# The zero fill of a table in DRAM: four transfers behind the constants, or one transfer ahead of everything

## The chip, the cores and the metric

The kernel runs on one core of one Trainium2 chip. The metric is the device time of one execution in microseconds (us), as the median of several runs. A kernel here is a program for five engines, each with its own queue of instructions in a fixed order: PE (matrix products), DVE and ACT (vector and scalar work), POOL (GpSimd), and SP, which only issues transfers. ACT and POOL issue transfers too. All transfers run on the core's 16 DMA engines, and the engines meet through semaphores.

## The reference, cut to what matters

The reference is two layers of a network on a graph: 1250 nodes with 512 channels, 40000 edges with 8 attributes each, one per head. The part that matters here is the attention of the first layer, whose scores between a source node s and a target node d get a bias from the edges between them:

```
table[s, d, 0:8] = sum over edges e = (s, d) of exp(edge_attr_8[e, :] - shift)
table[s, d, 8]   = number of edges (s, d)
```

Pairs without an edge must read as zero (the attention masks them). Ahead of the attention, and beside the building of this table, another branch of the layer is computed from x alone: normalization, K, V and Q products, linear attention, a small feed-forward part.

## The kernel before, in words

Nodes are padded to 1280, which gives ten tiles of 128. The table is `adj`, in DRAM, with one row of 9 floats for each of the 1280 x 1280 pairs (58.98 MB) and 896 spare rows for values that belong nowhere. It is used in three steps.

*Zero fill* (lines 221 to 228). POOL writes a row `zrow` of 128 x 1800 zeros. SP then issues four transfers, each of which writes that row 16 times for each of 128 partitions (14.4 thousand KB each), and a small one for the spare rows. In the program's text this stands behind the constants.

*Keys and weights* (lines 230 to 297). ACT loads `src`, `dst` and the edge attributes `wgt`. DVE makes a key `src * 1280 + dst` of each edge. PE turns the keys in three blocks, and ACT stores them in DRAM (`key_d`, line 269), from where they come back spread over all partitions (`kr`, line 311). ACT takes the exponential of `wgt` (line 283), and DVE splits the result into three bf16 parts `w` (line 290 and on).

*Scatter* (generator `scatter_edges`, lines 303 to 393). Groups of six columns of 128 edges are compared with each other by key (DVE, lines 325 and 335), PE sums the weights of equal keys (line 317), and POOL adds each column's sums to the table by an indirect DMA (line 351), 313 in all. The first group's keys come by ACT's queue, all later ones by SP's. The main program calls `pump(n)` to put n groups between its other work. A column's sums have 32 buffers, so that DVE and PE may run ahead of POOL.

The other branch (from line 481 on) begins with the loads of x in ten tiles, `xn` (line 487), the weights `L_mix_Wk` and `L_mix_Wv` and the bias rows, all issued by ACT. DVE normalizes the tiles, PE turns them (line 168) and makes the K and V products (line 179) and their product `kvps` (line 527). In PE's order the first group of the scatter stands ahead of most of these products, and the second group behind the last of them.

After the scatter the attention loads the table in slabs of 128 sources (`slab`, line 656), the first of which waits for the last two batches of scatters.

What sets the order around the zero fill: a scheduler places the instructions on each engine from the program's text, and the order within an engine is then fixed. Each transfer of SP or ACT is given one of eight completion semaphores (0 to 7), whichever engine issues it. A transfer that gets a semaphore that another transfer had before it waits, in its engine's queue, until that earlier one has landed, and what stands behind it in this queue waits with it. In the built program of this kernel the first zero transfer has semaphore 7, and the next transfer with this semaphore is ACT's third store to `key_d`; zero transfers 2 to 5 have semaphores 6, 1, 2 and 3, and the second follows ACT's first store to `xb_d` on semaphore 6.

Of the kernel before, what the change touches and what calls it, by code (L numbers as in the profile page):

```python
# [11 lines left out]
F32 = mybir.dt.float32  # L12
# [10 lines left out]
P = 128  # L23
N = 1250
NP = 1280
NT = NP // P
TAIL = N - (NT - 1) * P
C = 512
KC = C // P
# [4 lines left out]
EC = EF + 1  # L34
EREM = E - EF * P
B = 3
G = 2 * B
W3 = 3 * (H + 1)
CH = H + 1
NKEY = NP * NP  # L40
NROW = NKEY + (G + 1) * P
# [5 lines left out]
NEXP = 8  # L47
TOPK = 16
NKEYS = 256
# [17 lines left out]
def tile_gps_layers(ctx: ExitStack, tc: tile.TileContext, a, out):  # L67
    nc = tc.nc
# [4 lines left out]
    dram = ctx.enter_context(tc.tile_pool(name="dram", bufs=1, space=DRAM))  # L73
# [6 lines left out]

    def ps_tr(shape=(P, 512), name="tr"):
        return psum.tile(list(shape), F32, tag="tr", bufs=2, name=name)


    ident = const.tile([P, P], F32, name="ident")
# [61 lines left out]
    def norm_stats(pool, x_t, eps, name):  # L147

        st = pool.tile([P, 6], F32, tag="ln_st", name=name + "st")
        nc.vector.bn_stats(st, x_t)  # L150
        mv = pool.tile([P, 2], F32, tag="ln_mv", name=name + "mv")
        nc.vector.bn_aggr(mv, st)
        return mv[:, 0:1], rsqrt(pool, mv[:, 1:2], [P, 1], eps, name)
# [10 lines left out]
    def transposed(dst, tiles, t, gain=None, shift=None):  # L164

        ps = ps_tr((P, KC, P))
        for c in range(KC):
            nc.tensor.transpose(ps[:, c, :], tiles[:, c * P:(c + 1) * P], ident)
        to = dst[:, :, t * P:(t + 1) * P]
        if gain is None:  # L170
            nc.any.tensor_copy(to, ps)
        else:
            for c in range(KC):
                nc.vector.tensor_scalar(to[:, c, :], ps[:, c, :], col(gain, c), col(shift, c),
                                        op0=OP.mult, op1=OP.add)
# [9 lines left out]
    def nodes_of(t):  # L185
        return TAIL if t == NT - 1 else P
# [6 lines left out]
        mm(ps, [(w[:, c, m * P:(m + 1) * P], xT[:, c, c0:c0 + cn]) for c in range(xT.shape[1])])  # L193


    adj = dram.tile([NROW, CH], F32, name="adj")
    key_d = dram.tile([EC, P], F32, name="key_d")
    cnt_d = dram.tile([NP, NP], F32, name="cnt_d")
    q_d = dram.tile([P, KC, NP], F32, name="q_d")
    xm_d = dram.tile([NP, C], F32, name="xm_d")  # L200
    xb_d = dram.tile([NP, C], F32, name="xb_d")
    att_d = dram.tile([P, KC, NP], F32, name="att_d")
    deg_d = dram.tile([P, NP], F32, name="deg_d")
    w1f_d = dram.tile([NEXP, P, KC, 256], F32, name="w1f_d")
    wgd_d = dram.tile([P, KC, C], F32, name="wgd_d")
    wqd_d = dram.tile([P, KC, NKEYS], F32, name="wqd_d")
    bsum_d = dram.tile([P, C], F32, name="bsum_d")

    s_xn = ctx.enter_context(ExitStack())
    pxn = s_xn.enter_context(tc.tile_pool(name="xn", bufs=1, side="right"))
    xn = pxn.tile([P, NT, C], F32, tag="xn", name="xn")

    s_edge = ctx.enter_context(ExitStack())
    pe = s_edge.enter_context(tc.tile_pool(name="edge", bufs=1, side="right"))
    s_tmp = ctx.enter_context(ExitStack())
    ptmp = s_tmp.enter_context(tc.tile_pool(name="edgetmp", bufs=1, side="right"))

    zrow = pe.tile([P, 1800], F32, name="zrow")
    nc.gpsimd.memset(zrow, 0.0)
    adj_p = adj[0:NKEY, :].rearrange("(p r) c -> p (r c)", p=P)
    step = 16 * 1800
    for z0 in range(0, NKEY * CH // P, step):
        nc.sync.dma_start(adj_p[:, z0:z0 + step].rearrange("p (a f) -> p a f", f=1800),
                            zrow[:, None, :].to_broadcast([P, 16, 1800]))
    nc.sync.dma_start(adj[NKEY:NROW, :].rearrange("(p r) c -> p (r c)", p=P), zrow[:, :(G + 1) * CH])  # L228

    def edge_column(name, src, width, dt, fill):  # L230
        t = ptmp.tile([P, EC, width] if width > 1 else [P, EC], dt, name=name)
# [31 lines left out]
    for c0 in range(0, EC, P):  # L263
        cn = min(P, EC - c0)
        ps = ps_tr((P, P))
        nc.tensor.transpose(ps[:cn, :], key[:, c0:c0 + cn], ident)
        kt = ptmp.tile([P, P], F32, tag="kt", name="kt", bufs=2)
        nc.vector.tensor_copy(kt[:cn], ps[:cn, :])
        nc.scalar.dma_start(key_d[c0:c0 + cn, :], kt[:cn])


    mx = pe.tile([P, H], F32, name="mx")
    nc.vector.tensor_reduce(mx, wgt.rearrange("p j h -> p h j"), axis=AX.X, op=OP.max)
    ps = ps_tr((P, P))
    nc.tensor.transpose(ps[:H, :], mx, ident)
    mxt = pe.tile([H, 1], F32, name="mxt")
# [204 lines left out]
    with (tc.tile_pool(name="mix", bufs=1) as pm, tc.tile_pool(name="mixw", bufs=2) as pw,  # L481
# [99 lines left out]
        for t in range(NT):  # L581
            ps = ps_mm()
            node_mm(ps, hid, t, w2)
            f = pw.tile([P, C], F32, tag="f", name="f")
# [20 lines left out]
    with tc.tile_pool(name="gqkv", bufs=2) as pq:  # L605
# [5 lines left out]
        for t in range(NT):  # L611
            z = pq.tile([P, C], F32, tag="z", name="z")
            m, r = norm_stats(pq, xn[:, t, :], 1e-5, "lnz")
# [220 lines left out]
    def node_norm(pool, t, x_t, eps, name):  # L834

        st = pool.tile([P, 6], F32, tag="nn_st", name=name + "st")
        nc.vector.bn_stats(st, x_t)
        mv = pool.tile([P, 2], F32, tag="nn_mv", name=name + "mv")
        nc.vector.bn_aggr(mv, st)
        w = pool.tile([P, 1], F32, tag="nn_w", name=name + "w")  # L840
        nc.vector.tensor_scalar_add(w, mv[:, 1:2], eps)
        s = pool.tile([P, 1], F32, tag="nn_s", name=name + "s")
        nc.scalar.activation(s, w, AF.Sqrt)
        r = pool.tile([P, 2], F32, tag="nn_r", name=name + "r")
        nc.vector.reciprocal(r[:, 0:1], s)
        nc.vector.tensor_scalar(s, r[:, 0:1], r[:, 0:1], w, op0=OP.mult, op1=OP.mult)
        nc.vector.tensor_scalar(s, s, -0.5, 1.5, op0=OP.mult, op1=OP.add)
        nc.vector.tensor_scalar(r[:, 0:1], r[:, 0:1], s, None, op0=OP.mult)
        nc.vector.tensor_scalar(r[:, 1:2], mv[:, 0:1], r[:, 0:1], -1.0, op0=OP.mult, op1=OP.mult)
        return r  # L850

    with tc.tile_pool(name="gff", bufs=1) as pf, tc.tile_pool(name="gffw", bufs=2) as pw:
# [34 lines left out]
        with tc.manual_schedule(engines={nc.tensor.engine, nc.vector.engine, nc.scalar.engine}):  # L887
            for t in range(NT + 2):
                if t < NT:
# [7 lines left out]
                    r = node_norm(pw, t, X[:, t, :], 1e-5, "lnf")  # L897
# [24 lines left out]
            for c, (c0, cn) in enumerate(CHUNKS):  # L922
                n = cn // P
                for k, t in enumerate(range(c0 // P, c0 // P + n)):
# [4 lines left out]
                    r = nodes_of(t)  # L929
# [1068 lines left out]
```

## Time and profile before

| what | value |
|---|---|
| median of 3 runs | 2404.56 us (2402.94 to 2405.39) |
| the profiled execution, its own time | 2411.48 us |
| its span, first to last instruction | 2409.0 us |
| mean granted TensorE clock | 0.908 |
| PE busy | 1979.6 us (82%) |
| DVE busy | 1511.0 us (63%) |
| ACT busy | 808.2 us (34%) |
| POOL busy | 697.1 us (29%) |
| written to DRAM / read from it | 92.80 MB / 161.05 MB |

The span is that of one profiled execution; the median is of other runs, without the profiler. The profile shows the busy time of each engine, cut into 40 slices of the span, the costliest groups of instructions (line, engine, operation, output and inputs, how often; busy time and mean ns of one; idle time just ahead of them and what ended most of it), and a chain of waits, followed back from the last instruction to what released each step. Timelines list instructions in order of time: start, length, engine, line, operation, and in brackets the idle time ahead of it and what ended that. "SPq" and "ACTq" are the queues of these engines, in which transfers are issued[...].

### The profile page before, as it was taken

Reading aid. Unit: us, or ns where it says so; the run is one execution under the profiler, and the core shown is the slowest. Engines: PE = TensorE matmul, PEld = TensorE weight load, DVE = VectorE, ACT = ScalarE, POOL = GpSimd, SP = SyncE. Lnnn points to the kernel's source line nnn. Section 1 sums busy time; section 2 is a strip of 40 time slices with the busy share of each in tenths; the row PEclk is TensorE's granted clock in tenths of the full one; section 3 lists DMA queues with packets and bytes.
Section 4 is the critical chain, followed back from the end, with each engine's and each line's share of the span. In section 5 each row is a group of like instructions: output and inputs, shape, how many; then the busy total and the mean of one; then the engine's idle time right before and its main releaser. Section 6 shows DMA issues by size and latency. Waiting matters only on the chain.

```text
span 2409.0 us, 29786 instructions
## 1 busy us (share of the span) xinstructions
PE 1979.6 (82%) x10588; PEld 1180.5 (49%) x10588; DVE 1511.0 (63%) x4838; ACT 808.2 (34%) x1529; POOL 697.1 (29%) x448
## 2 busy tenths in 40 slices
PE   0767698885498499999789999999999999978943
PEld 0335475552244366666444546667445445555521
DVE  3717958879961399999561456656222242599998
ACT  0000011110230277677441156666111122244653
POOL 2006888888888100000000000000000000036665
PEclk9987798986599599999899999999999999989975
DMA  9898565444542665665250110000400101000000
GB/s 359 361 418 239 111 125 110 86 61 88 136 72 16 231 223 186 233 211 196 86 175 26 43 36 1 1 1 13 153 26 27 35 3 68 22 22 10 10 9 17
DMA packets 134385, 255.79 MB, mean 106 GB/s; under 512 B 51805, under 2 KB 90134, under 8 KB 132572
## 3 DMA queue, kind: packets, MB, share of 16 engines
q1 hardware_dynamic: 82368, 234.11, 26.3%
q0 software_dynamic: 46512, 8.02, 7.1%
q10 hardware_dynamic: 5356, 11.77, 1.3%
q8 instruction: 83, 1.36, 0.2%
q14 instruction: 66, 0.54, 0.1%
HBM read 161.05 MB, written 92.80 MB: 105 GB/s over the span
## 4 chain that ended last, share of the span: by engine, by line
PE 53%; DVE 23%; DMA 7%; ACT 6%; POOL 4%; issue 3%; SPq 3%; ACTq 0%; DVEq 0%; POOLq 0%
PE mm L179 26%; POOL adj L351 4%; PE sc L682 4%; PE one L731 4%; DVE eqx L335 4%; ACT wT L722 3%; DVE eq L325 3%; PE one L721 2%; DMA adj<-tot,idx 2%; PE ag L1382 2%; PE sc L1061 2%; PE av L1115 2%; PE one L1102 2%; SPq L228 2%; DMA adj<-zrow 2%
## 5 line engine op out<-in xcount | busy, mean ns | idle before, releaser
L351 POOL DMA_INDIRECT adj<-tot,idx x313 | 500.5, 1599 | 276.9 <-DMA kr<-key_d 180.1
L711 DVE SCALAR_TENSOR_TENSOR ex<-ex,slab 128x1280 f32<-128x1280 f32 x80 | 197.1, 2503 | 0.0
L325 DVE SCALAR_TENSOR_TENSOR eq<-kr,key,upto 128x128 bf16<-128x128 f32 (+2 forms) x313 | 145.3, 475 | 65.6 <-DMA kr<-key_d 40.0
L1313 DVE SCALAR_TENSOR_TENSOR X<-mm,gate,X 128x512 f32<-128x512 f32 x80 | 60.0, 750 | 196.9 <-PE mm L179 196.8
L335 DVE TENSOR_SCALAR_CACHE_REDUCE eqx<-kr,key 128x384 bf16<-128x384 f32 (+1 forms) x312 | 175.5, 599 | 0.8 <-PE even L317 0.8
L1251 POOL MEMSET padded<- 128x128 f32 x3 | 0.5, 204 | 543.0 <-DVE faT L1136 543.0
L722 ACT COPY wT<-one 128x512 f32<-128x512 f32 (+1 forms) x240 | 116.0, 516 | 96.8 <-PE one L721 92.5
L721 PE MATMUL one<-ident,ex 128*128 128x128 f32 x800 | 127.6, 289 | 23.5 <-ACT wT L722 19.7
L179 PE MATMUL mm<-w,hT 128*128 128x512 f32 (+1 forms) x320 | 144.3, 603 | 0.0
L179 PE MATMUL mm<-faT,w 128*128 128x512 f32 (+1 forms) x384 | 140.2, 518 | 0.7 <-ACT bs L1135 0.7
L682 PE MATMUL sc<-kT,q 64*128 64x512 f32 (+1 forms) x480 | 106.2, 566 | 40.9 <-DMA q<-q_d 38.6
L692 DVE CUSTOM_DVE_ANT_0 ex<-sc,none 128x1280 f32<-128x1280 f32 x80 | 115.7, 1485 | 17.4 <-PE sc L682 16.4
L721 PEld LDWEIGHTS one<-ident,ex 128*128 128x128 f32 x800 | 86.0, 143 | 66.8 <-ACT wT L722 48.2
L1075 DVE CUSTOM_DVE_ANT_0 ex<-sc,cmask 128x512 f32<-128x512 f32 (+3 forms) x144 | 72.9, 560 | 66.3 <-PE sc L1061 66.2
L704 ACT ACTIVATE ex<-ex,low 128x1280 f32<-128x1280 f32 x80 | 104.7, 1360 | 10.7 <-DVE low L697 10.7
L317 PEld LDWEIGHTS <-eq 128*128 128x128 bf16 x625 | 43.0, 103 | 132.3 <-DVE eq L325 96.0
L668 POOL DMA_DIRECT2D deg_d<-cnt x10 | 8.4, 844 | 340.2 <-ACT attT L738 319.6
L179 PEld LDWEIGHTS mm<-faT,w 128*128 128x128 f32 x384 | 73.3, 192 | 66.9 <-issue 65.9
L731 PE MATMUL one<-wT,gva 128*64 128x128 f32 x1600 | 103.0, 287 | 3.5 <-ACT wT L722 1.9
L1307 ACT ACTIVATE hT<-mm,cols 128x512 f32<-128x512 f32 (+1 forms) x48 | 29.0, 607 | 217.4 <-PE mm L179 217.4
L731 PEld LDWEIGHTS one<-wT,gva 128*64 128x64 f32 x1600 | 93.3, 145 | 13.5 <-ACT wT L722 13.5
L179 PEld LDWEIGHTS mm<-w,hT 128*128 128x128 f32 (+1 forms) x320 | 61.2, 192 | 75.6 <-issue 75.6
(493 smaller groups left out, 4090.7 us busy)
## 6 DMA issues: line engine op xcount, KB each, us to landing
adj<-zrow SPq DMA_DIRECT2D x4, 14400.0 KB
slab<-adj SPq DMA_DIRECT2D x10, 5760.0 KB, 17.3
kr<-key_d SPq DMA_DIRECT2D x50, 576.0 KB, 4.4
cnt_d<-cnt SPq DMA_DIRECT2D x10, 640.0 KB
deg_d<-cnt POOLq DMA_DIRECT2D x10, 640.0 KB, 7.0
adjT<-cnt_d SPq DMA_DIRECT2D x5, 1280.0 KB
adj<-tot,idx POOLq DMA_INDIRECT x313, 3.3
fw<-in_L_ffn_W SPq DMA_DIRECT2D x8, 512.0 KB, 3.9
```

The source lines that it names most:

```text
L179: nc.tensor.matmul(ps, lhsT=l, rhs=r, start=i == 0, stop=i == len(pairs) - 1)
L325: nc.vector.scalar_tensor_tensor(eq[:, :n], kr[:, k0 * P:k0 * P + n], key[:, c0 + c:c0 + c + 1], upto[:, B - 1 - c:, :].rearrange("p c x - ...
L335: nc.vector.tensor_scalar(eq[:, :n * P], kr[:, k0 * P:(k0 + n) * P], key[:, c0 + c:c0 + c + 1], None, op0=OP.is_equal, op1=OP.add, accum_o ...
L351: st = nc.gpsimd.indirect_dma_start(out=adj, out_offset=bass.IndirectOffsetOnAxis(ap=idx[:, c:c + 1], axis=0), in_=tot[:, c, :], in_offset ...
L682: nc.tensor.matmul(sc[e][:, d0:d0 + dn], lhsT=q[half(e), m, :], rhs=kT[half(e), m, d0:d0 + dn], start=True, stop=True)
L692: nc.vector.tensor_tensor_reduce(out=ex, in0=sc[e][:, :NP], in1=none, scale=-0.125, scalar=-LOWEST, op0=OP.add, op1=OP.min, accum_out=low[ ...
L704: nc.scalar.activation(exs[e], exs[e], AF.Exp, bias=low[:, e:e + 1], scale=-1.0)
L711: nc.vector.scalar_tensor_tensor(exs[e], exs[e], 1.0, sl[:, :, hd], op0=OP.mult, op1=OP.mult, accum_out=den[:, hd:hd + 1])
L721: nc.tensor.transpose(ps[:, k, :], weights[t, m][e][:, (d0 + k) * P:(d0 + k + 1) * P], ident)
L722: nc.scalar.copy(wT[:, d0:d0 + dn, :], ps[:, :dn])
L731: nc.tensor.matmul(av[half(e), 0, :], lhsT=va[:, d, hd * D:(hd + 1) * D], rhs=turned[e][:, d, :], start=d == 0, stop=d == NT - 1)
L1075: nc.vector.tensor_tensor_reduce(out=exs[e][:, d0:d0 + dn], in0=sc[k][e][:, :dn], in1=cmask[:, NP - n + d0:NP - n + d0 + dn], scale=-0.125 ...
```

## The change: what it does

The row `zrow` is written by DVE as its first instruction, the four transfers become one that SP issues, and the small one for the spare rows goes to ACT. All of this, with the DRAM tiles and the two pools that it needs, moves in the text ahead of the constants. The size of the table, the row and the number of bytes stay as they are.

```diff
+    zrow = pe.tile([P, 1800], F32, name="zrow")
+    nc.vector.memset(zrow, 0.0)
+    reps = NKEY * CH // P // 1800
+    nc.sync.dma_start(adj[0:NKEY, :].rearrange("(p r) c -> p (r c)", p=P).rearrange("p (a f) -> p a f", f=1800),
+                      zrow[:, None, :].to_broadcast([P, reps, 1800]))
+    nc.scalar.dma_start(adj[NKEY:NROW, :].rearrange("(p r) c -> p (r c)", p=P), zrow[:, :(G + 1) * CH])
+
     ident = const.tile([P, P], F32, name="ident")
     make_identity(nc, ident)
...
-    zrow = pe.tile([P, 1800], F32, name="zrow")
-    nc.gpsimd.memset(zrow, 0.0)
-    adj_p = adj[0:NKEY, :].rearrange("(p r) c -> p (r c)", p=P)
-    step = 16 * 1800
-    for z0 in range(0, NKEY * CH // P, step):
-        nc.sync.dma_start(adj_p[:, z0:z0 + step].rearrange("p (a f) -> p a f", f=1800),
-                            zrow[:, None, :].to_broadcast([P, 16, 1800]))
-    nc.sync.dma_start(adj[NKEY:NROW, :].rearrange("(p r) c -> p (r c)", p=P), zrow[:, :(G + 1) * CH])
```

In the built program the queues then begin as follows. SP: two loads `fw`, the zero transfer, the second and third group of keys `kr`, `peer_down`, `fw`, `gws`; the loads `gws`, `gnn_b` and `fb`, which stood ahead of the zero transfers, come later. ACT: `cols`, `src`, `dst`, `wgt`, the spare rows, the three ends of the edge arrays, eight tiles of x, two stores to `key_d`, two tiles of x, Wk, the third store to `key_d`, the exponential of `wgt`, Wv, the bias rows, the first `kr`. Before, the third to sixth of these were mixed with the ends, and the first two stores to `key_d` stood behind the third tile of x. The zero transfer has completion semaphore 6, and the next transfer with that semaphore is ACT's fourth tile of x. The spare rows have semaphore 7. All later orders, on every engine, are those of before but for neighbours that change places in the first groups.

More of the change, by code (lines that the diff above doesn't have):

```diff
@@ L82, in ps_tr @@
         return psum.tile(list(shape), F32, tag="tr", bufs=2, name=name)
+    adj = dram.tile([NROW, CH], F32, name="adj")
+    key_d = dram.tile([EC, P], F32, name="key_d")
+    cnt_d = dram.tile([NP, NP], F32, name="cnt_d")
+    q_d = dram.tile([P, KC, NP], F32, name="q_d")
+    xm_d = dram.tile([NP, C], F32, name="xm_d")
+    xb_d = dram.tile([NP, C], F32, name="xb_d")
+    att_d = dram.tile([P, KC, NP], F32, name="att_d")
+    deg_d = dram.tile([P, NP], F32, name="deg_d")
+    w1f_d = dram.tile([NEXP, P, KC, 256], F32, name="w1f_d")
+    wgd_d = dram.tile([P, KC, C], F32, name="wgd_d")
+    wqd_d = dram.tile([P, KC, NKEYS], F32, name="wqd_d")
+    bsum_d = dram.tile([P, C], F32, name="bsum_d")
+    s_xn = ctx.enter_context(ExitStack())
+    pxn = s_xn.enter_context(tc.tile_pool(name="xn", bufs=1, side="right"))
+    xn = pxn.tile([P, NT, C], F32, tag="xn", name="xn")
+    s_edge = ctx.enter_context(ExitStack())
+    pe = s_edge.enter_context(tc.tile_pool(name="edge", bufs=1, side="right"))
+    zrow = pe.tile([P, 1800], F32, name="zrow")
[4 more added lines that the diff above has]
+    nc.scalar.dma_start(adj[NKEY:NROW, :].rearrange("(p r) c -> p (r c)", p=P), zrow[:, :(G + 1) * CH])
     ident = const.tile([P, P], F32, name="ident")
@@ L193, in chan_mm @@
         mm(ps, [(w[:, c, m * P:(m + 1) * P], xT[:, c, c0:c0 + cn]) for c in range(xT.shape[1])])
[L196 to L217, printed above, removed]
     s_tmp = ctx.enter_context(ExitStack())
     ptmp = s_tmp.enter_context(tc.tile_pool(name="edgetmp", bufs=1, side="right"))
-    zrow = pe.tile([P, 1800], F32, name="zrow")
-    nc.gpsimd.memset(zrow, 0.0)
-    adj_p = adj[0:NKEY, :].rearrange("(p r) c -> p (r c)", p=P)
-    step = 16 * 1800
-    for z0 in range(0, NKEY * CH // P, step):
-        nc.sync.dma_start(adj_p[:, z0:z0 + step].rearrange("p (a f) -> p a f", f=1800),
-                            zrow[:, None, :].to_broadcast([P, 16, 1800]))
-    nc.sync.dma_start(adj[NKEY:NROW, :].rearrange("(p r) c -> p (r c)", p=P), zrow[:, :(G + 1) * CH])
     def edge_column(name, src, width, dt, fill):
```

## The prediction

> **What bounds the kernel now.** I read first the page's table of slices (who is busy when), then the page's costliest groups, then the chain of waits for the first 235 us, then the timelines of ACT, PE and POOL around the places where that chain turns.
>
> The slices (60.2 us each):
>
> ```profile
> PE   0767698885498499999789999999999999978943
> ...
> POOL 2006888888888100000000000000000000036665
> ...
> DMA  9898565444542665665250110000400101000000
> ```
>
> DMA is full in slices 1 to 4 (0 to 240 us), POOL is idle in slices 2 and 3 and then evenly busy in slices 4 to 13 (180 to 790 us), while PE has gaps. Slices 4 to 13 are the scatter: 313 indirect DMAs from POOL.
>
> ```profile
> L351 POOL DMA_INDIRECT adj<-tot,idx x313 | 500.5, 1599 | 276.9 <-DMA kr<-key_d 180.1
> ```
>
> 313 x 1.599 = 500.5 us busy; of the idle 276.9 us, 180.1 lie before the first one, and the other 96.8 are about 0.3 us ahead of each, by its timeline. So from first to last the scatter runs at 1.599 + 0.309 = 1.908 us each, back to back: whatever delays its feed early, and can't be worked off later by POOL, delays the attention stage behind it, whose first slab waits for the last scatters. The question is only what the change does to the start of POOL's unbroken run.
>
> The chain of waits, 0 to 235 us (start, length, what):
>
> ```profile
> 10.61 43.03 DMA adj<-zrow
> ...
> 56.84 2.30 ACT wgt L283
> ...
> 59.23 2.77 DVE w L290
> ...
> 122.06 48.99 SPq L228
> ...
> 171.23 22.98 DMA kr<-key_d
> ```
>
> The first zero transfer (14.7 MB) heads this chain, and what it releases is not a reader of the table but ACT's queue. ACT's timeline shows this (start, length, queue, line):
>
> ```profile
> 17.78 5.08 ACTq L487 DMA_DIRECT2D xn<-in_x  x5
> 53.71 0.50 ACTq L269 DMA_DIRECT2D key_d<-kt  x1
> ```
>
> From 22.9 to 53.7 ACT issues nothing: its next store is to use completion semaphore 7, which the first zero transfer still holds. Zero transfers 2 to 5 are issued from 77.6 on, and the keys kr behind them on SP land at 194.2. Meanwhile PE does its long block (K and V products, then kvps):
>
> ```profile
> 75.48 1.97 PE L168 MATMUL tr<-ident,xn 128*128 128x128 f32 x8 [50.55 <-DVE xn L157]
> ...
> 157.94 2.18 PE L527 MATMUL kvps<-va,kp 128*128 128x130 f32 x18
> 194.66 0.20 PE L317 MATMUL even<-w,eq 128*128 128x27 bf16 x1 [34.54 <-DVE eq L325]
> ```
>
> PE is done at 160.1 and stands for 34.5 us until the second group of keys is there. So the block lies wholly under the zero fill. POOL:
>
> ```profile
> 193.96 1.78 POOL L351 DMA_INDIRECT adj<-tot,idx  x1 [180.14 <-DMA kr<-key_d]
> ...
> 205.75 1.64 POOL L351 DMA_INDIRECT adj<-tot,idx  x1 [0.30 <-DVE eq L325]
> ```
>
> The first six scatters belong to the first group of keys, made before the block; the seventh (205.75) is the first whose sums come from PE after the block.
>
> **The change, part by part.**
>
> *The row of zeros from DVE.* POOL's memset of 128x1800 took 1.61 us. DVE's memsets took 0.17 us for 128 columns and 0.48 us for 512, so 0.8 ns a column: about 1.5 us, done near 2.4 us. POOL loses 1.6 us of work in a stretch where it later stands idle until 194; DVE gains 1.5 us in front of work that waits for loads until 7.0 (key from src_i). Both cost nothing; without that cover 1.5 us.
>
> *One transfer for four.* 58.98 MB either way. The Trainium skill (DMA: Bandwidth & Descriptors, Anatomy of one DMA) counts some 2 us fixed for each DMA of the POOL kind, by which one for four would win 6 us; but transfers 2 to 5 show no gap (DMA share 1.01 from 79 to 193 us), so by the row it wins 0, which I take. The new form (8192 rows on the table's side, 128x64 on the row's) isn't in the trace for zeros; the nearest are att_d<-attT, with the same uneven split, which hold SP's queue for 0.56 us against some 0.33 of others and land in 2.6 us for 256 KB. So issue costs 0.2 us more, at SP's front. SP is held while the engines' queues are full, as before's last two zero issues were (26.2 and 49.0 us). Behind it on SP stand kr, peer_down, fw, gws: all wait for later things anyway.
>
> *When it lands.* Issued near 2.5 us, it moves once the fw loads ahead of it on SP are through. Until it lands, the engines move 58.98 MB of zeros, 1.05 MB fw, 1.7 MB of edges and columns and three x loads (0.79 MB): 62.5 MB. The trace moved 0.9 MB by 5 us, 367 GB/s from 5 to 10, and 424 GB/s from 40 to 50 us when zeros ran alone (418 to 422 with x loads between). So 10 + (62.5 - 0.9 - 1.8) / 0.422 = 152 us. A rule speaks against this: the same page (Where 436 GB/s comes from) lets the HBM side bind at about 358 GB/s for a core. By it, the estimate is 62.5 / 0.358 = 175 us. The trace holds 412 GB/s over 79 to 193 us, so the row decides: 152. Before, the last zeros landed at 192.8 (122.06 + 70.7), since 25 us (53.6 to 79) had none in flight and 10 us passed ahead of the first. So the fill itself ends 41 us earlier.
>
> *What waits for it.* In the built program the big transfer uses completion semaphore 6, and ACT's fourth x load waits for that semaphore to reach 16, that is, for all 58.98 MB. ACT is in order. Behind this load stand six more x loads, all three key_d stores, Wk, the exponential of wgt, Wv, mixrows and the first kr. Before, only the third key_d store and what follows were held, and only to 53.7; now more is held, to 152. Everything that DVE and PE do from 59 us on waits for it.
>
> *From the release to the exponential.* Before: 53.66 to 59.13, 5.5 us. After: five x loads (0.41 us each by the pair at 54.26) and two key_d stores (0.5 each) come first, 3 us; the third block of keys reuses DVE's buffer and so waits for the first key_d store to land, some 2.5 us more by small transfers' landing times (2.0 to 2.6); then its issue, 1.3 us table load, 2.3 us exponential: 10 us, end at 162. Bounds 8 (store lands at once) and 14 (7 us, as under the old fill).
>
> *From the exponential to the end of PE's block.* 59.13 to 160.12 before: 101.0 us of DVE splitting w (14 us), norms, transposes and PE's 85 us at granted clock 1.00. PE's and DVE's orders there are the same but for swaps of neighbours. Nothing of it can start earlier, so 162 + 101 = 263. Less DMA traffic beside it could win a few us (0 to 5); I take 0, since PE's products follow each other without gaps from 98 to 158.
>
> *The second group of keys.* Its PE work still stands behind the block in PE's order, and DVE's behind the last va. The keys are there (kr on SP waits for an xb_d store, about 186), so DVE has its eq ready, and PE reaches the sums in 2 to 3 us: seventh scatter at about 263 + 2.7 = 265.8, against 205.75. In general the shift is landing + 10 + 101 + 2.7 - 205.75 = landing - 92, so 152 gives **+60 us**. The first six scatters, from about 188, are done by 200 and win nothing.
>
> *After that.* 307 scatters at the same rate. DVE and PE make three of them in 3.7 us (ten batches from 197.5 to 230.8), POOL needs 5.7, so the feed leads within one batch; before, the last sums were made at 726.7, 63 us ahead of POOL's last scatter. The slab issue goes from 792.6 to about 853. PE's own work of this stage ends at 771.5 + 68 = 840 (its second group moves from 194.7 to 263), ahead of its next need, the first score at 810 + 60. So the 60 us go through to the end.
>
> *Small moves.* The tail of the table from ACT (31.5 KB), gws, gnn_b and fb later on SP: under 0.5 us each, beside waits; 0.
>
> Sum: span 2409.0 + 60 = 2469, the profiled execution 2411.5 + 60 = 2471.5; the median of the runs lies 6.9 below that execution (2404.56 against 2411.48), so 2404.6 + 60 = **2465 us**.
>
> **The rivals.** *ACT isn't held* (the side of faster). If the fourth x load did not wait for the zeros, x, keys and the exponential would be through near 35 us, PE's block near 135, and POOL would start when the zeros land, at 154 instead of 194: -40 us, 2365. For it: the fill does end 41 us earlier, and the x loads before (13.7 us to landing) got through beside the zeros. Against it: the wait is in the built program, and the same kind of wait cost ACT 31 us before. It decides at landing = 92 us: a release before that makes the change free or better; 62.5 MB by then would need 680 GB/s. Chance 0.05; 0.02 more for no change.
>
> *The fill is slower.* The single uneven transfer goes to the engines less evenly, or the 358 GB/s hold: landing at 175 to 185, each us passed on: 2488 to 2498. For it: the form is new at this size. Against it: the att_d rows. Chance 0.11.
>
> *Part of the block is hidden.* POOL's run or the later stages win back 15 to 30 us (an earlier release of the first groups, less DMA beside PE): 2435 to 2450. Against it: POOL's pace is even to the end. Chance 0.08.
>
> The forecast itself 0.74, between 2450 and 2482: landing 148 to 158, release to exponential 8 to 14, PE's block up to 5 shorter. The range 2445 to 2491 leaves out the faster cases, half of the slowest and part of the hidden case. Faster 0.05, within 0.2% (about what a measurement can tell) 0.02, slower 0.93.
>
> **What would show it.** ACT's queue empty from about 15 to 152 us with the chain going through the zero transfer; the exponential near 160; PE idle to about 178 and its block to 263; POOL with six scatters near 188, a gap of some 65 us, and the rest even to 850. Wrong it would be if ACT issues its fourth x load early, if the big transfer lands far from 152, or if the scatters after the gap come faster than 1.9 us.

## The result: 2.7% slower, and the profile after

| kernel | median | range, runs |
|---|---|---|
| before | 2404.97 us | 2402.94 to 2408.21, 4 |
| after | 2473.36 us | 2471.54 to 2475.77, 4 |

The ratio of after to before is 1.0271, with a 95% interval from 1.0256 to 1.0285. The profiled execution of after took 2473.14 us with a span of 2471.4. The profiled execution of before, which the prediction starts from, was itself 6.5 us above the median of its runs, so that the two profiles differ by 62 us and the medians by 68.

The slices of after (61.8 us each, rows of the page as before):

```profile
PE   0009969888559679999969999999999999978853
POOL 1001588888888600000000000000000000045665
DMA  9981556543454365665270110000400002000000
GB/s 397 418 314 54 148 108 126 114 84 64 88 130 73 68 244 194 230 243 192 91 247 9 45 50 1 1 1 2 151 26 34 26 9 69 22 22 8 10 9 17
```

The zero fill is over in slice 3 now: 397, 418 and 314 GB/s, then 54. But PE, which had begun to work in slice 2, does nothing in slices 1 to 3, and POOL's even run has moved back by one slice. The fill came earlier and everything else later. In the costliest groups the row of the scatter says the same:

```profile
L350 POOL DMA_INDIRECT adj<-tot,idx x313 | 499.4, 1595 | 342.4 <-DMA xb_d<-xn 180.0
```

Each scatter costs what it did (1595 ns against 1599). Idle time ahead of them is 342.4 us against 276.9, 65.5 more. ACT's timeline shows where the delay begins (start, length, queue):

```profile
7.36 148.31 ACTq L486 DMA_DIRECT2D xn<-in_x  x8
155.77 0.87 ACTq L268 DMA_DIRECT2D key_d<-kt  x2
...
161.10 0.28 ACTq L268 DMA_DIRECT2D key_d<-kt  x1
...
162.70 2.29 ACT L282 ACTIVATE wgt<-wgt 128x2504 f32<-128x2504 f32 x1
```

Eight loads of x stretch over 148 us: three go out by 13.6, the fourth at 153.4, when the zeros have landed. The chain of waits has this as one piece, and then the block (start, length, what):

```profile
13.63 139.75 another core or an unknown queue
157.17 4.21 DMA xn<-in_x
162.70 2.30 ACT wgt L282
...
204.48 55.79 PE mm L207 x130
...
264.85 2.01 PE kvps L526 x18
```

"Unknown queue" is a reading aid worth keeping: the kernel has one core, and no instruction of it runs in these 139.75 us on the chain. It is ACT's queue, waiting on the completion semaphore that its fourth load of x shares with SP's transfer; the profile has no name for such a wait. POOL at the other end:

```profile
192.09 1.78 POOL L350 DMA_INDIRECT adj<-tot,idx  x1 [179.98 <-DMA xb_d<-xn]
...
203.33 1.68 POOL L350 DMA_INDIRECT adj<-tot,idx  x1 [0.31 <-issue]
267.86 1.54 POOL L350 DMA_INDIRECT adj<-tot,idx  x1 [62.85 <-DVE idx L347]
```

Six scatters, then a hole of 62.85 us until DVE's indices for the seventh, which stand behind PE's block. The seventh starts at 267.86 against 205.75, the last at 852.4 against 789.6.

### The profile page after: what moved, and what is told of

It reads as the page before. It is cut to its first block, busy times and chain, and to the rows that moved or that the text cites. A ratio compares the mean times of both kernels' runs of the same rounds, so it can differ in the third digit from the quotient of the medians.

```text
span 2471.4 us, 29782 instructions
## 1 busy us (share of the span) xinstructions
PE 1977.5 (80%) x10588; PEld 1176.5 (48%) x10588; DVE 1513.0 (61%) x4838; ACT 809.4 (33%) x1530; POOL 694.3 (28%) x447
## 4 chain that ended last, share of the span: by engine, by line
PE 56%; DVE 24%; ACT 7%; another core or an unknown queue 6%; DMA 3%; issue 2%; POOL 2%; ACTq 0%; SPq 0%; DVEq 0%; POOLq 0%
PE mm L207 31%; DVE eqx L334 4%; PE sc L681 4%; PE one L730 3%; ACT wT L721 3%; DVE eq L324 3%; PE ag L1381 2%; PE sc L1060 2%; PE one L720 2%; PE av L1114 2%; PE one L1101 2%; POOL adj L350 2%; DVE sc L1741 2%; DMA adj<-tot,idx 1%
## 5 line engine op out<-in xcount | busy, mean ns | idle before, releaser
L350 POOL DMA_INDIRECT adj<-tot,idx x313 | 499.4, 1595 | 342.4 <-DMA xb_d<-xn 180.0
L1312 DVE SCALAR_TENSOR_TENSOR X<-mm,gate,X 128x512 f32<-128x512 f32 x80 | 60.0, 750 | 199.5 <-PE mm L207 199.4
L196 PE MATMUL tr<-ident,xn 128*128 128x128 f32 x40 | 7.2, 319 | 154.2 <-DVE xn L185 154.2
L703 ACT ACTIVATE ex<-ex,low 128x1280 f32<-128x1280 f32 x80 | 104.8, 1360 | 11.6 <-DVE low L696 11.6
L730 PEld LDWEIGHTS one<-wT,gva 128*64 128x64 f32 x1600 | 88.5, 139 | 13.7 <-ACT wT L721 13.7
```

The lines of the kernel that those rows point to most:

```text
L350: st = nc.gpsimd.indirect_dma_start(out=adj, out_offset=bass.IndirectOffsetOnAxis(ap=idx[:, c:c + 1], axis=0), in_=tot[:, c, :], in_offset ...
L703: nc.scalar.activation(exs[e], exs[e], AF.Exp, bias=low[:, e:e + 1], scale=-1.0)
L730: nc.tensor.matmul(av[half(e), 0, :], lhsT=va[:, d, hd * D:(hd + 1) * D], rhs=turned[e][:, d, :], start=d == 0, stop=d == NT - 1)
```

## The experiments

The theory: the fill's completion semaphore holds ACT's queue until it lands, and from the release a fixed path of about 114 us (loads, exponential, PE's block) leads to the seventh scatter. Its rivals: that a fill in front is slow for the loads because they share the 16 DMA engines, whichever semaphore it has; and that the place in front, or DVE's row, is what costs. In the table, "seventh" and "last" are the starts of these scatters in the profile, "experts" is the time from the gate of the experts' stage (L1274 in after) to that stage's last sum (L1312), which is needed below. Ratios are to runs of before on the same chip, with the 95% interval. The runs were made in five groups, in which the medians of before were 2404.97, 2408.58, 2407.95, 2411.06 and 2407.38 us, so kernels of different groups are compared by their ratios and not by their medians.

| kernel | seventh | last | experts | span | median | ratio |
|---|---|---|---|---|---|---|
| before | 205.75 | 789.6 | 285.2 | 2409.0 | 2404.97 | |
| before_again | 205.55 | 789.5 | 285.2 | 2405.5 | 2408.08 | 0.9999 (0.9989 to 1.0009) |
| after | 267.86 | 852.4 | 288.8 | 2471.4 | 2473.36 | 1.0271 (1.0256 to 1.0285) |
| after_again | 268.47 | 852.5 | 288.0 | 2471.9 | 2471.75 | 1.0251 (1.0236 to 1.0267) |
| one_old_place | 267.79 | 850.8 | 285.1 | 2468.6 | 2469.63 | 1.0261 (1.0244 to 1.0279) |
| three_and_one | 232.91 | 816.6 | 285.2 | 2436.4 | 2438.57 | 1.0133 (1.0106 to 1.0159) |
| two_halves | 208.75 | 789.6 | 287.9 | 2407.6 | 2411.44 | 1.0013 (1.0000 to 1.0025) |
| split_front | 197.62 | 778.9 | 288.0 | 2400.7 | 2402.80 | 0.9977 (0.9969 to 0.9985) |
| dve_row | 199.39 | 782.8 | 285.2 | 2400.7 | 2403.10 | 0.9982 (0.9973 to 0.9990) |
| pool_old | 206.66 | 791.1 | 288.0 | 2413.6 | 2414.71 | 1.0024 (1.0013 to 1.0034) |
| loads_by_pool | 190.30 | 777.4 | 285.1 | 2394.7 | 2396.72 | 0.9949 (0.9931 to 0.9968) |
| store_late | 183.63 | 776.3 | 285.1 | 2394.8 | 2396.12 | 0.9939 (0.9926 to 0.9951) |
| store_late_act | 183.94 | 771.5 | 288.1 | 2392.4 | 2393.68 | 0.9935 (0.9921 to 0.9950) |

Line numbers differ by one to three between the kernels.

### How much of the fill stands in the way: split_front, two_halves, three_and_one

All three are the changed kernel, with the fill in front cut into pieces. The first piece has completion semaphore 6, and ACT's fourth load of x waits for that piece alone. The pieces behind it wait, in SP's queue, for later transfers of ACT: in two_halves and three_and_one the second piece has semaphore 6 again, and in split_front the other three have semaphores 2, 7 and 0.

```diff
-    reps = NKEY * CH // P // 1800
-    nc.sync.dma_start(adj[0:NKEY, :].rearrange("(p r) c -> p (r c)", p=P).rearrange("p (a f) -> p a f", f=1800),
-                      zrow[:, None, :].to_broadcast([P, reps, 1800]))
+    adj_p = adj[0:NKEY, :].rearrange("(p r) c -> p (r c)", p=P).rearrange("p (a f) -> p a f", f=1800)
+    for a0, a1 in ((0, 32), (32, 64)):        # three_and_one: (0, 48), (48, 64); split_front: four of 16
+        nc.sync.dma_start(adj_p[:, a0:a1, :], zrow[:, None, :].to_broadcast([P, a1 - a0, 1800]))
```

> The changed kernel, but with the four transfers of before in place of the one (row by DVE, all in front). If the length of the transfer on completion semaphore 6 is what costs: only the first quarter stands there, it lands at about 40 to 46 us, ACT is let go then, the K and V block ends at about 155 to 160, the last quarter lands at about 185, so scatters start at about 185 instead of 192 and the seventh follows at once: shift about -7 to -20 against before, about 2390 to 2398 us. If the place in front of all loads, or the row by DVE, is what costs: ACT would be late here too and the time stays at 2465 us or above.

> The changed kernel with the one transfer cut into two halves, the first in front with completion semaphore 6, the second behind it on SP (it waits until that semaphore has also counted ACT's third store of xb_d, at about 106 us). Theory (ACT is free when the transfer on semaphore 6 lands, 101 us of block and 10 to 12 us of start follow): half of the fill lands at about 80, the block ends at about 193 instead of 267, the second half lands at about 185: the time falls by about 74 against the changed kernel, to about 2396 to 2402 us. Rival (any fill in front delays the loads by sharing the DMA engines, whichever semaphore it has): the same bytes are moved, so 2450 us or more.

> The changed kernel with three quarters of the fill in the transfer in front (semaphore 6) and the last quarter behind it. Theory: the first part lands at about 118, ACT is free then, the block ends at about 231; the quarter runs beside the block and lands before 231: the time is half way, about 35 us under the changed kernel and about 26 to 33 over before, 2431 to 2438 us. Together with the halves it gives a slope of one us of time for each us of landing. Rival (sharing of the DMA engines): 2450 us or more, and no slope.

The chain of waits of three_and_one:

```profile
14.09 104.04 another core or an unknown queue
...
127.19 2.30 ACT wgt L282
...
169.53 55.79 PE mm L207 x130
```

Its POOL, by the timeline, around the hole:

```profile
206.04 1.55 POOL L350 DMA_INDIRECT adj<-tot,idx  x1 [0.31 <-issue]
232.91 1.54 POOL L350 DMA_INDIRECT adj<-tot,idx  x1 [25.32 <-DVE idx L347]
```

It has the same picture as after with every number smaller: release at 14.09 + 104.04 = 118.1 instead of 153.4, and the seventh scatter at 232.9 instead of 267.9. The release came 35.3 us earlier and the seventh scatter 35.0 earlier; the hole on POOL shrank from 62.85 to 25.32. From release to seventh it is 114.8 us here and 114.5 in after. So the slope of one that the theory asks for is there, between these two points. The median, 2438.6, was half a us outside what was expected (2431 to 2438).

In two_halves the release came at 83.0:

```profile
13.89 69.06 another core or an unknown queue
...
134.64 55.81 PE mm L207 x130
...
191.16 7.06 another core or an unknown queue
```

By 114.5 us of path the seventh would come at 197.5. It came at 208.75, because now the table itself was late: the first scatter started only at 197.4, when the second half had landed, and the second unknown piece of the chain is the wait for it. That half was issued at 118.0, since it waits for semaphore 6 once more, behind ACT's third store of xb_d. I had reckoned with about 106 for that and a landing at 185. So the expected 2396 to 2402 was missed by 9 us, for a reason of the same kind as the loss under study, and the point says little about the slope.

In split_front the two costs part for good:

```profile
2.78 44.86 DMA adj<-zrow
...
103.78 55.81 PE mm L209 x130
...
160.30 26.50 another core or an unknown queue
```

Release at 47.6, PE's products done by 160, and then 26.5 us in which the table is waited for: scatters from 186.3 on without a hole. So the place in front and DVE's row cost nothing by themselves; the last scatter is 10.6 us earlier than in before_again. Of these, 5 us reached the span and about 5.5 the time; the experts' stage was 3 us longer (below), the attention stage 2.6. That is less than expected (2390 to 2398), but the rival's 2465 is out.

### Merging without moving: one_old_place

The kernel before, with one transfer in the old place, the row by POOL.

> The kernel before with the four transfers made one in the old place, row by POOL. The transfer then has completion semaphore 7, and the issue of ACT that waits for it is the third store of key_d, after the x loads and Wk. Theory (merging costs, not the place): the fill lands at about 156, the exp of the edge attributes behind that store starts at about 160, the block ends at about 263 and the time is about 2465 to 2470 us. Rival (the place in front costs, because the x loads come late): here the x loads go out early, so the time stays within 10 us of before, 2395 to 2415 us.

Measured: 2469.63, as the theory had it. The chain of this kernel:

```profile
24.53 134.97 another core or an unknown queue
162.70 2.30 ACT wgt L281
...
204.41 55.79 PE mm L179 x130
```

ACT's timeline around that wait:

```profile
18.09 6.44 ACTq L485 DMA_DIRECT2D xn<-in_x  x5
159.57 0.50 ACTq L267 DMA_DIRECT2D key_d<-kt  x1
```

Here eight loads of x are out by 24.5, beside the fill. It is ACT's third store of key_d that waits, until 159.5, and behind it two x loads, Wk and the exponential. The fill landed 6 us later than in after, but the way from release to exponential took 3 us in place of 9, and both exponentials start at 162.70. So making four transfers one is the loss, to within 2 us (the last scatter is at 850.8 against 852.4 in after); placing it in front gains some us of landing and gives them back in ACT's queue.

### Is it the semaphore, or the sharing of the engines: loads_by_pool

The changed kernel, fill untouched; ACT's loads behind the first few, and the stores of xb_d, are issued by POOL, whose transfers have semaphores of their own.

```diff
-            nc.scalar.dma_start(xn[:n, t, :], a["x"][t * P:t * P + n, :])
-        wk = load_w(pm, "L0_mix_Wk", KC, C, bufs=2, eng=nc.scalar)
+            nc.gpsimd.dma_start(xn[:n, t, :], a["x"][t * P:t * P + n, :])
+        wk = load_w(pm, "L0_mix_Wk", KC, C, bufs=2, eng=nc.gpsimd)
...
-            nc.scalar.dma_start(xb_d[t * P:(t + 1) * P, :], xn[:, t, :])
+            nc.gpsimd.dma_start(xb_d[t * P:(t + 1) * P, :], xn[:, t, :])
```

The ends of the edge arrays, Wv and the bias rows in the same way.

> The changed kernel, with the one transfer where it is, but ACT's loads of x, Wk, Wv and mixrows, the tails of the edge arrays and the stores of xb_d issued by POOL, which counts its transfers on semaphores of its own: no issue of ACT now waits for the transfer's semaphore. Theory (the semaphore that SP's and ACT's transfers share is what holds ACT): ACT and the block of K and V are free of the fill, it lands at about 160 to 175 beside the loads, and scatters start there without the pause after the sixth: about 2380 to 2400 us. Rival (a transfer of 59 MB in front starves the loads of the same 16 DMA engines, or ACT's queue is held by something other than the semaphore): x and the weights land after about 140 again, the block ends at about 260 and the time stays at 2460 to 2475 us.

Measured: 2396.72, faster than both kernels. ACT's exponential is at 26.6 us instead of 162.7, and the chain now reads:

```profile
47.28 12.84 DMA kr<-key_d
...
78.16 57.52 PE mm L207 x134
136.40 43.00 another core or an unknown queue
```

PE's long run of products went from 78 to 136 (the first ones at 50) beside the same 59 MB transfer, and then the table was waited for until 179. The same fill from the same queue at the same time, with the loads sharing the engines, costs nothing here, where nobody's queue meets its semaphore. That settles the theory against sharing. The edit takes most of ACT's transfers away, so one could still ask whether a fill in flight blocks ACT's queue as a whole. It doesn't: beside the fill ACT issued stores of key_d at 21.9 and 30.3 in this kernel, and the last five of those eight loads in one_old_place, by 24.5. What stands is a single instruction, and each time it is the next one with the semaphore of the first zero transfer: the third store of key_d in before and one_old_place (semaphore 7), the fourth load of x in after and the fifth in dve_row (semaphore 6). This run also shows what sharing does cost: with the loads moving beside it, the fill lands at 179 instead of 153.

### The fill on POOL's own queue: pool_old

The other way round: the kernel before with one transfer, issued by POOL in the old place, the spare rows too.

```diff
-        nc.sync.dma_start(adj_p[:, z0:z0 + step]...
+    nc.gpsimd.dma_start(adj[0:NKEY, :]..., zrow[:, None, :].to_broadcast([P, reps, 1800]))
```

> The kernel before, with its four transfers made one and issued by POOL in the old place, behind its own row of zeros; the spare rows by POOL too. POOL's transfers are counted on semaphores of its own, so neither SP nor ACT waits for the fill. Theory: the fill runs beside the loads, lands at about 165 to 175, scatters start there: about 2380 to 2400 us. Rivals: POOL [...]is held for so long that scatters start no earlier than 192 (about 2405 us); or one long transfer starves the loads whatever queue it has (2440 us or more).

Measured: 2414.71, slower than before by 0.24%; the theory's number was wrong. POOL was not held for long (its issue took 2.9 us), nor was ACT up to its exponential, which is at 36.2. But loads were slow beside the fill, as the chain shows:

```profile
43.29 47.31 DMA mixrows<-in_mix_rows
...
111.61 58.37 PE mm L179 x136
172.27 19.07 DMA fw<-in_L_ffn_Wo
```

The bias rows (2 MB) took 47 us from their issue at 43.3, and PE's long run of products began at 112, 33 us later than in loads_by_pool; then PE, in order, stood 19.2 us for half a MB of `fw` before the rest of the block. The first scatter came at 195.2. So the second rival, sharing, held here in part.

Two differences between the versions bear on these 33 us. In pool_old the scheduler put DVE's work on the bias rows ahead of the normalization of x, and DVE stood 34.6 us for them, until 90.6; in loads_by_pool that work stands behind most of it, and DVE didn't wait for the rows. And the loads were slower in themselves. From 28 to 48 us the queue of the fill and the queue of the loads moved equally many packets in both versions (777 and 777 in loads_by_pool, 929 and 932 in pool_old), but the loads got 2.73 MB through with theirs in loads_by_pool and 1.60 MB in pool_old: their packets were smaller, 1.7 KB on average against 3.5. Why they were smaller on ACT's queue, and how the 33 us divide between the two, stays open.

### The row alone: dve_row

```diff
-    nc.gpsimd.memset(zrow, 0.0)
+    nc.vector.memset(zrow, 0.0)
```

> The kernel before, with only the row of zeros written by DVE in place of POOL; four transfers in the old place. The first then stands in SP's queue about 7 us earlier and has semaphore 6, so ACT's x load that waits for it is held until about 45 us instead of issuing at once. Theory (the row's engine is worth nothing by itself): within 8 us of before on either side, 2397 to 2410 us. Rival (the row by DVE is a part of the loss): over 2415 us.

Measured: 2403.10, inside the range. It is 4 to 5 us better: the first zero transfer is issued at 2.9 instead of 10.6 us, and the seventh scatter comes some 6 us earlier. As expected, the fifth load of x stands for the first zero transfer, from 13.7 to 48.3. The row's engine has no part in the loss.

### A second profile of each kernel: before_again, after_again

> The kernel before, unchanged. Its profiled execution stood 6.5 us above the median of its own runs; the shift of 62 us between the two profiles is 6 us under the 68 us between the medians. If that profile was an outlier, this one spans about 2401 to 2404 us and is shorter behind the scatters (the stage after the last scatter to the last score), with scatters starting at 192 and ending at about 790 again; if not, it spans about 2409 again, and the 6 us are in the executions without a profile.

> The changed kernel, unchanged, beside the same runs of before as the version above. If the 62 us by which the scatters moved are the whole effect, its median is 62 to 64 us over that of before; the two medians so far stood 68 us apart, and the second profile of before has a span 66 us under that of the changed kernel: then 65 to 68 us, of which 3 to 4 us lie in the experts stage, where some matmuls ran at a lower granted clock.

The second span of before is 2405.5, between the two that were expected, with scatters to 789.5 as in the first. From the first score to the last it took 348.1 us against 353.5; that stage differs from execution to execution (347 to 354 in these profiles). Against this profile, after is 65.9 us longer, and the scatters account for 62.9. Another 3.6 lie in the experts' stage, 288.8 us against 285.2. They go with the granted clock. Two windows of that stage, of before_again: its first long run of products, and the one with the 20 small products `degr` (window, length, then busy time of PE, PEld, DVE, ACT and POOL, granted clock, DMA share, GB/s):

```profile
1712.00:1854.00 142.00, 142.00 (x366) 69.14 (x365) 32.28 (x43) 15.88 (x25) 0.00 (x0) 0.99 0.09 30
1854.00:1861.00 7.00, 5.22 (x46) 4.45 (x45) 2.41 (x12) 0.77 (x2) 0.00 (x0) 1.00 0.00 1
```

The same windows of after:

```profile
1774.50:1918.00 143.50, 143.50 (x366) 69.63 (x365) 32.27 (x43) 15.88 (x25) 0.00 (x0) 0.98 0.09 30
1918.00:1926.00 8.00, 6.22 (x45) 4.93 (x44) 2.40 (x11) 0.57 (x2) 0.00 (x0) 0.79 0.00 1
```

The same 366 products take 1.5 us longer, at 0.98 instead of 0.99; the window of `degr` is 1 us longer, at 0.79 instead of 1.00; and nearly 1 us is lost between the gate and these windows, where the clock is 0.56 instead of 0.69. Behind `degr` the stage runs alike. The `degr` products take 273 ns each in one case and 421 in the other, and the 13 profiles have one or the other: 421 in after, after_again, split_front, two_halves, pool_old and store_late_act, 273 in the rest. Where they take 421, the stage is some 3 us longer (see the table). Each of the two kernels with two profiles had the same both times, though kernels with the same start of the stage differ (its gate is at 1698.4 in before_again and at 1698.2 in two_halves). What decides it stays open.

The medians of after_again and of before beside it differ by 60.7 us (2471.75 against 2411.06; by the interval, 57 to 64), where 65 to 68 was expected; the first two differed by 68.4 (62 to 68.5). So the 3 us of the clock are seen in the profiles, but the medians don't show them: those of before alone ran from 2405 to 2411 from one group of runs to the next, and a shift of 62 to 64 us is within both intervals.

### What bounds the start then: store_late, store_late_act

In loads_by_pool the scatters wait for the fill to land, with the DMA engines full. Moving bytes away from in front of that should bring it forward.

```diff
-            nc.scalar.activation(z, xn[:, t, :], AF.Identity, scale=r, bias=b)
+            za = nc.scalar.activation(z, xn[:, t, :], AF.Identity, scale=r, bias=b)
...
-            nc.gpsimd.dma_start(xb_d[t * P:(t + 1) * P, :], xn[:, t, :])
+            st = nc.gpsimd.dma_start(xb_d[t * P:(t + 1) * P, :], xn[:, t, :])     # store_late_act: nc.scalar
+            tc.add_manual_dep(st.ins, za.ins.name, SYNC, reason="the table first")
```

> The version with ACT's loads and stores issued by POOL, with the ten stores of xb_d (256 KB each, 2.6 MB) in addition made to follow the activation that reads the same tile much later. There the fill landed at about 179 us, and the 16 DMA engines moved 415 to 425 GB/s without a gap until 175 us. Theory (with ACT free, the bytes in front of the fill's end set the start of the scatters): 2.6 MB at 420 GB/s are 6 us, the fill lands at about 173, scatters start there, about 2389 to 2392 us, some 6 us under the version with the stores early. Rival (the start is bound by something other than the bytes): no change, 2395 to 2399 us.

The first scatter came at 172.3, 6.7 us earlier, as reckoned. But the last came only 1.1 us earlier, and the time stayed (ratio 0.9939 against 0.9949, within both intervals). The stores went to where POOL has no slack; the row of the tile xb_d in store_late (count, shortest/median/longest in ns, first and last start):

```profile
L622 POOL DMA_DIRECT2D xb_d<-xn x10: 1105/1164/1201, 681.6 to 702.0; - x10
```

Ten stores of 1.16 us, all among the last scatters.

> As the version with the late stores of xb_d, but these ten stores are issued by ACT behind its own activation of the same tile, not by POOL. With POOL issuing them, the scatters started 6.7 us earlier (172.3 against 179.0) and ended only 1.1 us earlier (776.3 against 777.4), and the time stayed. Theory (the stores' own 1.16 us each on POOL stood between scatters and took the gain back): now the scatters start at about 172, end at about 770, and the time is about 6 us under both of those versions, 2389 to 2392 us. Rival (something else stretches the scatter run): they end at about 776 again, 2395 to 2398 us.

With ACT issuing them, the last scatter is at 771.5, 5.9 us earlier than in loads_by_pool, so the stores on POOL were what had taken it. The median, 2393.68, is 2 us above what was expected, and this kernel ran its experts' stage at the lower clock, 288.1 us. It is 0.65% under before (0.50 to 0.79%). That is the lowest ratio here, but its interval overlaps those of store_late and loads_by_pool: the 5.9 us are shown in the scatters and not in the time.

## Why the prediction was right

The forecast was 2465 us and slower, the measurement 2473.4 with an interval for the ratio that excludes no change by far. By its steps:

- *The row from DVE, one transfer for four, small moves: nothing.* Right. DVE's memset took 1.56 us (reckoned 1.5), and dve_row shows that it is no cost.
- *SP is held while the engines' queues are full.* Not for this issue: that of all 8192 rows took 0.64 us. Before's last two zero issues had stood for 26 and 49, but the last of them was the 31.5 KB of spare rows, behind four large transfers, so that time was not a matter of its own size. SP issued nothing more until 187.8, when the fill had landed, so the step had no effect, and whether a transfer behind the fill would have stood wasn't seen in after.
- *Landing at 152.* It was 153.4. The rate was 397 to 418 GB/s over the first two slices, so the trace's row was the right one to choose, and the 358 GB/s of the Trainium skill (DMA: Bandwidth & Descriptors, Where 436 GB/s comes from), by which the estimate was 175, didn't bind here.
- *What waits for it.* Right: ACT's fourth x load, by semaphore 6. This was read from the built program, and loads_by_pool, with the other kernels in which the held instruction changes with the semaphore, shows that it is the cause.
- *Release to the end of the exponential, 10 us.* It was 11.6 (153.4 to 165.0): the third store of key_d didn't go out until 161.1, after Wk.
- *From there to the end of PE's block, 101 us.* 101.9 (to 266.9). It is the same work at the same granted clock, 1.00 over PE's block in both profiles.
- *Seventh scatter 2.7 us later.* 1.0, since DVE had its comparisons ready.
- *Shift 60 us, all of it passed on.* 62.1 at the seventh scatter, 62.8 at the last. POOL's run was as even as before, and between three_and_one and after the seventh scatter moves with the release, 35.0 us for 35.3.

So the mechanism was right, and the shift of the scatters was 2 to 3 us short. That it was so close is in part luck: the landing (1.4 us), the way to the exponential (1.6) and the block (0.9) were all taken too short, and 1.7 us too much for the seventh scatter gave back nearly half. The other 6 us of the 8 by which 2465 was missed aren't settled. Some 3 may be the experts' clock, which the profiles of after have and which nothing in the profile of before announced. The rest, and perhaps all of it, is in the medians themselves: beside another group of runs of before the difference was 60.7 us, not 68.4.

The rival that would have been faster, "ACT isn't held", was given -40 us. The runs that set ACT free, or nearly so, show that this was too much: loads_by_pool gained 11 us and split_front 5.5. It let the fill land at 154 while the loads moved too, but the bytes of the loads are then in front of its end as well, and it lands at 179. Its deciding point, a release by 92 us, lies between two_halves (83, no change) and three_and_one (118, 1.3% slower), but two_halves was held by its late second half, so the point itself isn't tested.

## What to carry to other kernels

In a program built like this one, a long transfer holds more than its reader: it holds whatever queue next draws its completion semaphore, and everything in order behind that. Before making transfers fewer and larger, list which instruction on each queue waits next on their semaphores and what stands behind it; four transfers of 15 MB did here what one of 59 MB couldn't, because the first was done at 54 us. Then look at what bounds the start once the queue is free: here it was the bytes in front of the fill's end, and a store moved out of their way may not land on the engine that has no slack.

## What was not expected of the hardware

- One transfer of 8192 rows of 7.2 KB was issued by SP in 0.64 us, and the engines moved 397 to 418 GB/s while it ran; before's smaller ones had no advantage in rate (412 GB/s from 79 to 193 us).
- A fill of 59 MB and the loads beside it moved equally many packets (777 and 777, or 929 and 932, in 20 us), whichever of the two was on POOL's queue. The loads got a share of the bytes by the size of their packets: 2.73 MB in one case, 1.60 MB in the other. With the fill on POOL's queue a load of 2 MB on ACT's took 47 us and one of half a MB on SP's 19 us.
- The same 20 products ran at 273 ns in some kernels and at 421 in others, with the clock at 1.00 and 0.79 in the window around them, the same in both profiles of before and of after.
